# Issue order of DMAs in two recurrent scan layers: pinned loads and writes, a corner block in two parts on two queues, a block's older rows loaded first

## The chip, the cores and the metric

The kernel runs on one core of a Trainium2 chip. The metric is the device time of one execution in microseconds (us). The engines are TensorE (PE, matrix multiplications), VectorE (DVE), ScalarE (ACT), GpSimd (POOL) and SyncE (SP). SP and ACT also issue DMAs, each from its own queue: an issue that waits holds up everything behind it in the same queue.

## The reference, cut to what matters

The input is (4, 48, 256, 256) in float32: batch, channels, rows, columns. Four residual layers follow one another; the change touches the last two, which have the same form:

```python
def layer(x):                                   # layers 2 and 3 of the reference
    v = gn(x)                                   # group norm, 16 groups
    # conv1d: width 5, 48 channels to 48, along the other axis, with a bias
    # down: rows 0 to 255
    D[0] = v[:, :, 0];  D[h] = v[:, :, h] + conv1d(D[h - 1], down_w)
    # up: back over D, with the same weights; the last row of D stands in twice
    seq = rows 253, 252, ..., 0 of D, then row 255
    U = scan over seq from D[255], then reversed
    # right: columns 0 to 255 of U;  left: back over R
    R[0] = U[..., 0];   R[w] = U[..., w] + conv1d(R[w - 1], right_w)
    L[255] = R[255];    L[w] = R[w] + conv1d(L[w + 1], left_w)
    return x + L
```

Each layer is thus four chains of 255 steps, and a step needs the one before it.

## The kernel before, in words

The function `scans` does both scan layers; in its loop `layer` is 0 and 1. Layers 0 and 1 of the reference lie ahead of it and are not touched.

**A step.** A row (or column) of the image is kept as three blocks of 128 partitions by 128 elements: 8 positions times 48 channels are 384 lines, and the 128 elements are 32 groups of positions times the batch of 4. `step` (matmuls at L1227, additions at L1233) computes the convolution as nine 128x128 matmuls in float32, each of which the profile records as two, and adds the bias and the new input by three DVE operations.

**Tiles.** Eight rows make one row tile `D[a]`, a from 0 to 31, 1.5 MB. Three ring buffers and three slots hold row tiles in turn; the last five stay in the chip's memory, all others are written to memory by SP (L1371) at the end of their row tile, and come back for the up scan (L1428). `R[t_]` are the tiles of eight columns in the right scan, written likewise and read back by ACT's queue (L1582) in the left scan. Two big tiles hold, in turn, a block's input `x`, the corner and column blocks `u` and `c`, and the stage `s`.

**Down.** The input of a row tile is made by `norms`: twelve scale-and-shift operations, on ACT at L1302 (for the very first row tile a part goes to DVE and POOL, L1300). It writes them straight into the ring that the row tile will use: the norms of D[a+1] are issued among the steps of row tile a. With three rings in turn, that ring is free when D[a-2] has been written to memory. The scale and shift come from the group norm's statistics: `bn_stats` at L1569 in layer 0's left scan, gathered at L1596, averaged by L1603 and L1610, a Sqrt at L1615, and `spread` at L1244. The input x of four row tiles is a block J. Block J+1 is loaded from row tile 4J on: in layer 0 by `load_x2` (12 transfers), in layer 1 by `load_y` (L1263), ten transfers of rows of 256 bytes, 6.3 MB. The ten pieces arise because a position's 48 channels can lie across two blocks of 128 partitions: 48, 48, 32, 16, 48, 48, 16, 32, 48 and 48 lines.

**Up, and the corner to right.** While the up scan runs, ACT copies every row into a column-ordered tile `u` (`keep_row`, L1383), and every 32 rows SP writes it to `U` (`write_U`, L1388, ten pieces). The right scan reads columns: `load_C` brings 32 columns of all rows. For the first 32 columns, rows 64 and up are loaded at row 40 (24 transfers, L1401), and the row block 32 to 63 (J0 = 1) at row 32 (three transfers, L1396). After the very last step the kernel writes the first 64 of the 512 elements per position of the last row block (ten pieces), loads them back (three transfers, L1396), writes the other 448, and loads the weights of left (L1211). POOL copies each column from `c` into place (`fetch`, L1444), and the first step of right waits for it.

**Left, and the crossing to layer 1.** In the left scan POOL adds each finished column to the residual in the stage tile (`add_line`, L1512). In layer 0 the stage is written to `Y1` by `write_Y` (L1517), a block n of 32 columns at a time, n falling from 7 to 0; for n = 0 it is done in two parts, the first 64 elements of each position (through SP, ACT, SP), then the other 448. Layer 1's first block needs all of Y1's blocks for its 32 rows: `look_ahead` issues the part of n = 1 to 7 (56 rows of 256 bytes per line) as soon as a big tile is free and block 1 is written, and the part of n = 0 (8 rows per line) comes after the first corner write, over both queues. In layer 1 the finished stage goes to `out` (L1558).

**What sets the order.** The code is handed to a scheduler that orders each engine's instructions by its own reckoning of readiness. `pin = tc.keep_in_program_order` marks those instructions that must keep the order in which the program issues them; before the change these are the matmuls and additions of `step`, and norms and copies, but no DMA. A DMA of SP or ACT is therefore placed by the scheduler, which can differ from the program: the transfers of row 32 and the weights of left, for instance, stand in SP's queue ahead of the corner's writes. All DMAs of both queues share eight semaphores in turn, so that each also waits for the one eight before it.

Of the kernel before, what the change touches and what calls it, by code (L numbers as in the profile page):

```python
# [10 lines left out]
AF = mybir.ActivationFunctionType  # L11
# [5 lines left out]
B, C, H, W = 4, 48, 256, 256  # L17
# [9 lines left out]
NPOS = 8  # L27
# [1125 lines left out]
def scans(ctx, tc, x2r, out, wts, biases, dram, k, coef2, spare):  # L1153
# [16 lines left out]
    nc = tc.nc  # L1170
# [13 lines left out]
    pieces = pieces_of_lines()  # L1184
    chunk = lambda m: slice(128 * m, 128 * m + 128)

    NBK = 8
    pin = tc.keep_in_program_order
# [8 lines left out]
    def big_tile(name):  # L1197
        return big_of.take(name)
# [5 lines left out]
    ways = [(layer, way) for layer in range(2) for way in range(3)]  # L1204
    weights = {}

    def load_weights(at):
        if at < len(ways):
            layer, way = ways[at]
            t = wp.tile([128, 9, 128], F32, tag="w", name="w")  # L1210
            nc.sync.dma_start(t.rearrange("p a b -> p (a b)"), wts[layer][way])  # L1211
            weights[layer, way] = t

    def step(w, bias, old, new, inp, then=()):
# [43 lines left out]
    def load_y(t, J, n0=0, n1=NBK, queues=(nc.sync,)):  # L1258
        v = t.rearrange("p (m q e) -> p m q e", m=3, e=64)
        src = Y1.rearrange("q c e -> c q e")  # L1260
        for q, (j, c0, c1, m, p0, np_) in enumerate(pieces):
            at = 512 * j + 64 * J
            queues[q % len(queues)].dma_start(  # L1263
                v[p0 : p0 + np_, m, 8 * n0 : 8 * n1], src[c0:c1, 8 * n0 : 8 * n1, at : at + 64]
            )

    load_x2(xin, 0)
# [2 lines left out]
    both = (nc.sync, nc.scalar)  # L1270
    coefs = spread(coef2[:C].rearrange("p b s -> p (b s)"), "spread0")

    for layer in range(2):
        bias = b_sb[layer]
        w = weights[layer, 0]
        slot_of_row = (lambda i: (i % 2) * 4 + i // 2) if layer == 0 else (lambda i: i)
        U = dram.tile([NPOS, 3 * 128, NBK, NBK * 64], F32, tag=f"U{layer}", name="U")
        Dd = [dram.tile([128, RING], F32, tag=f"D{layer}_{a}", name="D") for a in range(32)]
        Rd = [dram.tile([128, RING], F32, tag=f"R{layer}_{a}", name="R") for a in range(32)]
        flat = lambda t: t.rearrange("p i m n -> p (i m n)")  # L1280
# [59 lines left out]
        for a in range(32):  # L1340
            t, h = D[a]
            J, al = a // 4, a % 4
            if al == 0:
                if J > 0:
                    give(xin_h)
                    xin, xin_h = xnext
                if J + 1 < NBK:
                    xnext = big_tile("x")
                    if layer == 0:
                        load_x2(xnext[0], J + 1)  # L1350
                    else:
                        load_y(xnext[0], J + 1)
            todo = []
            if a + 1 < 32:
                D[a + 1] = ring_tile("d")
                todo = norms(D[a + 1][0], xin if al < 3 else xnext[0], (al + 1) % 4)
            if layer == 0 and al == 0:
                copy_rows(xin, J)
            if a == 24:
                load_weights(ways.index((layer, 1)))  # L1360
            for i in range(NPOS):
                line = t[:, slot_of_row(i)]
                if prev is not None:
                    step(w, bias[:, 0], prev, line, line)
                prev = line
                for piece in todo[3 * i // 2 : 3 * (i + 1) // 2]:
                    piece()
                if copies and i % 2 == 0:
                    copies.pop(0)()
            if a < 32 - KEEP:  # L1370
                nc.sync.dma_start(Dd[a], flat(t))  # L1371
                give(D.pop(a)[1])
        give(xin_h)

# [3 lines left out]
        ut = uh = None  # L1378
        near = None
# [2 lines left out]
            v = t.rearrange("p (m i n a) -> p m i n a", m=3, i=NPOS, a=4)  # L1382
            nc.scalar.copy(v[:, :, i, :, al], line)  # L1383

        def write_U(t, J, lo, hi):
            v = t.rearrange("p (m i e) -> p m i e", m=3, i=NPOS)
            for j, c0, c1, m, p0, np_ in pieces:
                nc.sync.dma_start(  # L1388
                    U[j].rearrange("(i c) J e -> c i J e", c=C)[c0:c1, :, J, lo:hi], v[p0 : p0 + np_, m, :, lo:hi]
                )  # L1390

        def load_C(t, n, J0, J1):
            v = t.rearrange("p (m j J e) -> p m j J e", m=3, j=NPOS, J=NBK)
            for m in range(3):
                if J1 - J0 == 1:
                    nc.sync.dma_start(  # L1396
                        v[:, m, :, J0, :], U[:, chunk(m), J0, n * 64 : n * 64 + 64].rearrange("j f e -> f j e")
                    )
                    continue
                for j in range(NPOS):  # L1400
                    nc.sync.dma_start(v[:, m, j, J0:J1, :], U[j, chunk(m), J0:J1, n * 64 : n * 64 + 64])  # L1401

        for a in reversed(range(32)):
            t, h = D.pop(a)
            for i in reversed(range(NPOS)):
# [5 lines left out]
                if row % 32 == 31:  # L1411
                    ut, uh = big_tile("u")
# [7 lines left out]
                if row == 40:  # L1420
                    near = big_tile("c")
# [6 lines left out]
                nc.sync.dma_start(flat(D[a - KEEP][0]), Dd[a - KEEP])  # L1428
        step(w, bias[:, 0], prev, last, last)
        keep_row(ut, 0, 0, last)  # L1430
        write_U(ut, 0, 0, 64)
        load_C(near[0], 0, 0, 1)
        write_U(ut, 0, 64, 512)
        give(uh)
        load_weights(ways.index((layer, 2)))


        w = weights[layer, 1]
# [24 lines left out]
        for t_ in range(32):  # L1463
            n, gl = t_ // 4, t_ % 4
            if t_ > 0:
                R[t_] = ring_tile("r", (slot_of, ring_of) if t_ in (24, 25, 26, 30, 31) else (ring_of, slot_of))
            t, h = R[t_]
            if gl == 0 and n + 1 < NBK:
                near = big_tile("c")
# [12 lines left out]
            if t_ < 32 - KEEP:  # L1482
                nc.sync.dma_start(Rd[t_], flat(t))
                give(R.pop(t_)[1])
        load_weights(ways.index((layer, 2)) + 1)


        w = weights[layer, 2]
# [25 lines left out]
        def write_Y(s, n, lo=0, hi=512, queues=(nc.sync,)):  # L1514
            dst = Y1.rearrange("(n i) c e -> n (i c) e", n=NBK)[n, :, :SLOT].rearrange("f (j e) -> f j e", j=NPOS)
            for m in range(3):
                queues[m % len(queues)].dma_start(  # L1517
                    dst[chunk(m), :, lo:hi], s[m].rearrange("p (j e) -> p j e", j=NPOS)[:, :, lo:hi]
                )

        stages = {NBK - 1: stage_of(NBK - 1)}
        if layer == 0:
# [12 lines left out]

        look_ahead()
        for t_ in reversed(range(32)):
            n, gl = t_ // 4, t_ % 4
            t, h = R.pop(t_)
            for j in reversed(range(NPOS)):  # L1540
                wc = 8 * t_ + j
                wl = wc % 32
                line = t[:, j]
                then = [stats.pop(0)] if stats else []
                if wc < 255:
                    step(w, bias[:, 2], prev, line, line, then)
                prev = line
                add_line(stages[n][0], wl, line)
                if done and not stats:
                    for hh in done.pop(0):  # L1550
                        give(hh)
                    look_ahead()
                s, hs = stages[n]
                if layer == 1 and wl < NPOS and (wl % 2 == 0 or wc < 2):
                    to = 1 if wc < 2 else 2
                    for m in range(3):
                        here = slice(512 * wl, 512 * (wl + to))
                        nc.sync.dma_start(out[n, chunk(m), here], s[m][:, here])  # L1558
                    if wl == 0:
                        for hh in hs:  # L1560
                            give(hh)
                if layer == 0 and wl % 16 == 0:
                    half = wl // 16
                    for m in range(3):
                        for b in range(B):

                            def stat(m=m, b=b, s=s, at=2 * n + half, half=half):
                                v = s[m].rearrange("p (q b e) -> p q b e", b=B, e=16)[:, :, b]
                                return nc.vector.bn_stats(parts[:, m, b, at, :], v[:, :, 8 * half : 8 * half + 8])  # L1569

                            stats.append(stat)
                    if half == 0:
                        if n > 0:
                            write_Y(s, n)
                            written.append(n)
                        done.append(hs)
            give(h)
            look_ahead()
            while ring_of.free and min(R, default=t_) > 0:
                new = min(R, default=t_) - 1  # L1580
                R[new] = ring_tile("r")
                nc.scalar.dma_start(flat(R[new][0]), Rd[new])  # L1582
        for f in stats:
            f()
        if layer == 0:
# [11 lines left out]
            mean = work.tile([C, 2 * B], F32, tag="mean", name="mean")  # L1597
            av = k["avg24", 128].rearrange("p (m c) -> p m c", m=3)

            def average(src, dst, cols):  # L1600
                ps = small.tile([C, B], F32, tag="small", name="pavg")
                for m in range(3):
                    nc.tensor.matmul(ps, lhsT=av[:, m], rhs=src[:, m], start=m == 0, stop=m == 2)  # L1603
                return ps
# [6 lines left out]
            dev = work.tile([128, 3, B], F32, tag="dev", name="dev")  # L1611
            nc.vector.tensor_sub(dev, mv[:, :, :, 0], ps)
            nc.vector.tensor_mul(dev, dev, dev)
            nc.vector.tensor_add(dev, dev, mv[:, :, :, 1])
            nc.scalar.activation(mean[:, B:], average(dev, None, B), AF.Sqrt, bias=k.eps[:C])  # L1615
            nc.vector.reciprocal(gc[:, :, 0], mean[:, B:])
            nc.vector.scalar_tensor_tensor(gc[:, :, 1], mean[:, :B], -1.0, gc[:, :, 0], ALU.mult, ALU.mult)
            coefs = spread(gc.rearrange("p b s -> p (b s)"), "spread1")
# [167 lines left out]
```

## Time and profile before

| what | value |
|---|---|
| three runs | 6930.88, 6943.6, 6946.01 us; median 6943.6 |
| the profiled execution | 6936.42 us, its span 6934.4 |
| PE busy | 6569.4 us (95% of the span), 55772 matmuls recorded |
| DVE, ACT, POOL busy | 3636.3, 1844.0, 2069.2 us |
| scan matmuls at L1227 | 18360 records on d at 276 ns each, 18360 on r at 276 ns |
| additions at L1233 | 348 ns each |
| stages (us of the span) | layer 0: down and up 2614.6 to 3641.0, corner to 3659.5, right and left to 4729.6; crossing to 4775.4; layer 1: down and up to 5881.4, corner to 5900.6, right and left to 6927.4 |

The span runs from the first to the last instruction recorded; the execution's own time has 2.0 us more around it. In an answer of the timeline each line gives the start in us, the time in us, the engine, the line of the kernel, the operation with output and input by the program's names, and how many. "SPq" and "ACTq" stand for the queue of an engine: there the time is how long issues took, not how long the transfers did. The chain is followed back from the last instruction: at each step to what released it. A busy PE is not a PE at its peak, and idle time on an engine that is not on the chain costs nothing.

### The profile page before, as it was taken

How to read it: one execution, taken by the hardware profiler on the slowest of the kernel's cores; microseconds unless marked ns; L12 is line 12 of the kernel's file. 1: busy time of each engine (PE TensorE's matmuls, PEld its weight loads, DVE VectorE, ACT ScalarE, POOL GpSimd, SP SyncE). 2: the span in 40 equal slices, each digit the busy share in tenths (PEclk: the TensorE clock that was granted, in tenths of full speed). 3: DMA queues.
4: the chain of work that ended last, by engine and by line, in shares of the span. 5: the costliest groups of instructions: out<-in, count | busy, mean ns of one | idle time of the engine just before them, and what ended most of it. 6: DMA issues, size and time to landing. Idle time of an engine off the chain costs nothing.

```text
span 6934.4 us, 133567 instructions
## 1 busy us (share of the span) xinstructions
PE 6569.4 (95%) x55772; PEld 5266.6 (76%) x55772; DVE 3636.3 (52%) x8740; ACT 1844.0 (27%) x2166; POOL 2069.2 (30%) x4211
## 2 busy tenths in 40 slices
PE   6999999999999779999998999986899999999999
PEld 4666633333333229999998999986899999999999
DVE  7777533555556554444444446754444444444444
ACT  3430022444444434444440000001544443000000
POOL 0000000233333554420004557652000000555777
PEclk9999999999999879999999999998999999999999
DMA  7742145677777769984669678989995566865775
GB/s 237 185 136 84 61 133 176 165 199 195 196 199 184 158 148 301 287 245 155 187 179 226 195 172 205 248 243 188 182 183 95 170 195 171 235 186 168 276 300 201
DMA packets 1177469, 1326.21 MB, mean 191 GB/s; under 512 B 831040, under 2 KB 1005760, under 8 KB 1124512
## 3 DMA queue, kind: packets, MB, share of 16 engines
q1 hardware_dynamic: 1163696, 1229.16, 65.4%
q10 hardware_dynamic: 13072, 88.18, 3.7%
q8 instruction: 437, 7.16, 0.4%
q14 instruction: 168, 1.38, 0.1%
q0 software_dynamic: 96, 0.33, 0.0%
HBM read 794.28 MB, written 522.19 MB: 190 GB/s over the span
## 4 chain that ended last, share of the span: by engine, by line
PE 86%; DVE 4%; DMA 3%; SPq 2%; ACT 2%; POOL 1%; issue 1%; ACTq 0%; POOLq 0%; DVEq 0%
PE ps L1227 57%; PE py L701 9%; PE acc L374 8%; PE py L710 5%; SPq L1263 2%; PE ph L830 2%; PE pout L1018 1%; PE psp L975 1%; DMA D<-d 1%; ACT d L1302 1%; POOL s L1512 1%; PE ptok L890 1%; DVE y L724 0%; DVE st L726 0%; DVE y L1027 0%
## 5 line engine op out<-in xcount | busy, mean ns | idle before, releaser
L1227 PE MATMUL ps<-d,w 128*128 128x128 f32 (+1 forms) x18360 | 2073.8, 276 | 104.3 <-DVE d L1233 61.1
L1227 PEld LDWEIGHTS ps<-d,w 128*128 128x128 f32 x18360 | 2069.2, 193 | 108.8 <-DVE d L1233 64.7
L1227 PE MATMUL ps<-r,w 128*128 128x128 f32 (+1 forms) x18360 | 2066.7, 276 | 68.7 <-POOL r L1444 36.0
L1227 PEld LDWEIGHTS ps<-r,w 128*128 128x128 f32 x18360 | 2064.6, 193 | 70.9 <-POOL r L1444 37.0
L1233 DVE SCALAR_TENSOR_TENSOR d<-ps,b,d 128x128 f32<-128x128 f32 x3054 | 979.7, 348 | 1155.4 <-PE ps L1227 1077.2
L1512 POOL TENSOR_TENSOR s<-s,r 128x128 f32<-128x128 f32 x1536 | 745.4, 521 | 334.3 <-DVE r L1233 331.0
L1233 DVE SCALAR_TENSOR_TENSOR r<-ps,b,pre 128x128 f32<-128x128 f32 x1530 | 490.3, 348 | 577.1 <-PE ps L1227 569.0
L1233 DVE SCALAR_TENSOR_TENSOR r<-ps,b,r 128x128 f32<-128x128 f32 x1530 | 490.1, 348 | 459.1 <-PE ps L1227 431.4
L374 PE MATMUL acc<-moving,raw 128*32 128x240 f32 (+1 forms) x6144 | 685.6, 381 | 12.3 <-DVE moving L357 11.5
L1444 POOL COPY pre<-c 128x128 f32<-128x128 f32 x1530 | 558.4, 404 | 464.3 <-DVE r L1233 462.5
L701 PE MATMUL py<-x1n,wy 128*96 128x512 f32 x1536 | 691.6, 599 | 0.0
L374 PE MATMUL acc<-moving,still 128*32 128x240 f32 (+1 forms) x6144 | 682.5, 381 | 6.8 <-DVE still L361 2.7
L1302 ACT ACTIVATE d<-x,spread 128x256 f32<-128x256 f32 x752 | 510.9, 824 | 550.2 <-DMA D<-d 380.6
L1383 ACT COPY u<-d 128x384 f32<-128x384 f32 x510 | 448.5, 900 | 573.5 <-DVE d L1233 541.0
L374 PEld LDWEIGHTS acc<-moving,raw 128*32 128x32 f32 x6144 | 430.0, 110 | 213.6 <-DVE moving L357 11.8
L701 PEld LDWEIGHTS py<-x1n,wy 128*96 128x96 f32 x1536 | 242.0, 163 | 410.8 <-issue 376.3
L1444 POOL COPY r<-c 128x128 f32<-128x128 f32 x6 | 2.4, 393 | 1691.2 <-DMA c<-U 1691.2
L724 DVE TENSOR_TENSOR y<-py,t 96x512 f32<-96x512 f32 x256 | 173.6, 678 | 462.1 <-PE py L710 462.0
L374 PEld LDWEIGHTS acc<-moving,still 128*32 128x32 f32 x6144 | 345.0, 110 | 34.7 <-issue 4.6
L710 PE MATMUL py<-x2n,wy 64*96 64x512 f32 x1536 | 360.8, 601 | 0.0
L1034 POOL COPY yr<-y 96x256 f32<-96x256 f32 x512 | 307.2, 648 | 129.4 <-DVE y L1027 128.4
L654 ACT ACTIVATE x1n<-t,g 128x2048 f32<-128x2048 f32 x64 | 134.2, 2096 | 696.1 <-PE py L701 573.9
(219 smaller groups left out, 4076.2 us busy)
## 6 DMA issues: line engine op xcount, KB each, us to landing
t<-in_xc SPq DMA_DIRECT2D x64, 1536.0 KB
c<-U SPq DMA_DIRECT2D x348, 256.0 KB
D<-d SPq DMA_DIRECT2D x54, 1536.0 KB
d<-D SPq DMA_DIRECT2D x54, 1536.0 KB
R<-r SPq DMA_DIRECT2D x54, 1536.0 KB
r<-R ACTq DMA_DIRECT2D x54, 1536.0 KB
U<-u SPq DMA_DIRECT2D x84, 768.0 KB
raw<-in_xp SPq DMA_DIRECT2D x36, 1728.0 KB
```

Source lines behind the costliest of these rows:

```text
L374: nc.tensor.matmul(out[32 * i : 32 * i + 32, : n * C], lhsT=still[i][:, first : first + 32], rhs=moving[:, i, lo : lo + n * C], start=u == ...
L701: nc.tensor.matmul(ps, lhsT=held["w"][0][:, dx], rhs=x1n[:, 2 * c : 2 * c + 2, dx : dx + W], start=dx == 0, stop=False)
L710: nc.tensor.matmul(held["ps"][q + 2 * s], lhsT=held["w"][1][here, dx], rhs=x2n[here, 2 * q : 2 * q + 2, dx : dx + W], start=False, stop=dx ...
L724: nc.vector.tensor_add(part, held["ps"][c], t1[:P, 2 * c : 2 * c + 2, :])
L830: nc.tensor.matmul(out[32 * q : 32 * q + 32], lhsT=w1_sb[:, half, i, :], rhs=moving(t), start=i < 4, stop=i >= 4)
L1034: made = nc.gpsimd.tensor_copy(yrs[c][:, :, 2 * i2 + ip, :].rearrange("p j (n a g) -> p j n a g", a=4, g=4)[:, :, :, al], y[:, i2, al].rea ...
L1227: nc.tensor.matmul(ps[m][:, here], lhsT=w[:, n, :], rhs=old[:, q, there], start=first, stop=last)
L1233: nc.vector.scalar_tensor_tensor(new[:, m], ps[m], bias[:, m : m + 1], inp[:, m], ALU.add, ALU.add)
L1302: pin(nc.scalar.activation(dst, src, AF.Identity, bias=g[:, 1:2], scale=g[:, 0:1]))
L1383: nc.scalar.copy(v[:, :, i, :, al], line)
L1444: nc.gpsimd.tensor_copy(dst[:, m].rearrange("p (J a b) -> p J a b", J=NBK, b=B), v[:, m, j, :, gl].rearrange("p J b a -> p J a b"),)
L1512: nc.gpsimd.tensor_add(v, v, line[:, m].rearrange("p (J a b) -> p J a b", J=NBK, b=B))
```

## The change

The change adds `pin` to a number of DMA issues and moves some of them. Weights: every `load_weights` is pinned; left's are issued in tile 2 of the right scan instead of ahead of it, and the next layer's in tile 29 of the left scan instead of ahead of it. Corner: `write_U` and the three-transfer form of `load_C` are pinned; the last writes go over SP and ACT in turn; the load that follows them is in two parts, positions 0 and 1 over ACT, SP, ACT, then positions 2 to 7 over SP, ACT, SP. Layer 1's down scan: the pieces of `load_y` and, in layer 1 alone, the D writes are pinned, so that SP issues them as the program has them: the ten pieces for block J+1 at the start of row tile 4J, then the write of D[4J] at its end. Crossing: the 56-row pieces, the writes of n = 0 and the 8-row pieces are pinned in the program's order, and so is the Sqrt of the statistics, which stands behind ACT's pieces there. In the pinned order the three transfers for the row block 32 to 63 go out at row 32, as the program has it.

```diff
@@ load_weights
-            nc.sync.dma_start(t.rearrange("p a b -> p (a b)"), wts[layer][way])
+            pin(nc.sync.dma_start(t.rearrange("p a b -> p (a b)"), wts[layer][way]))
@@ load_y
-            queues[q % len(queues)].dma_start(
-                v[p0 : p0 + np_, m, 8 * n0 : 8 * n1], src[c0:c1, 8 * n0 : 8 * n1, at : at + 64]
+            pin(
+                queues[q % len(queues)].dma_start(
+                    v[p0 : p0 + np_, m, 8 * n0 : 8 * n1], src[c0:c1, 8 * n0 : 8 * n1, at : at + 64]
+                )
             )
@@ down scan, end of a row tile
             if a < 32 - KEEP:
-                nc.sync.dma_start(Dd[a], flat(t))
+                made = nc.sync.dma_start(Dd[a], flat(t))
+                if layer == 1:
+                    pin(made)
                 give(D.pop(a)[1])
@@ write_U
-        def write_U(t, J, lo, hi):
+        def write_U(t, J, lo, hi, which=pieces, queues=(nc.sync,)):
             v = t.rearrange("p (m i e) -> p m i e", m=3, i=NPOS)
-            for j, c0, c1, m, p0, np_ in pieces:
-                nc.sync.dma_start(
-                    U[j].rearrange("(i c) J e -> c i J e", c=C)[c0:c1, :, J, lo:hi], v[p0 : p0 + np_, m, :, lo:hi]
+            for q, (j, c0, c1, m, p0, np_) in enumerate(which):
+                pin(
+                    queues[q % len(queues)].dma_start(
+                        U[j].rearrange("(i c) J e -> c i J e", c=C)[c0:c1, :, J, lo:hi], v[p0 : p0 + np_, m, :, lo:hi]
+                    )
                 )
@@ load_C
-        def load_C(t, n, J0, J1):
+        def load_C(t, n, J0, J1, j0=0, j1=NPOS, queues=(nc.sync,)):
             v = t.rearrange("p (m j J e) -> p m j J e", m=3, j=NPOS, J=NBK)
             for m in range(3):
+                queue = queues[m % len(queues)]
                 if J1 - J0 == 1:
-                    nc.sync.dma_start(
-                        v[:, m, :, J0, :], U[:, chunk(m), J0, n * 64 : n * 64 + 64].rearrange("j f e -> f j e")
+                    pin(
+                        queue.dma_start(
+                            v[:, m, j0:j1, J0, :],
+                            U[j0:j1, chunk(m), J0, n * 64 : n * 64 + 64].rearrange("j f e -> f j e"),
+                        )
                     )
                     continue
@@ after the last step of up
         keep_row(ut, 0, 0, last)
-        write_U(ut, 0, 0, 64)
-        load_C(near[0], 0, 0, 1)
+        write_U(ut, 0, 0, 64, pieces, both)
+        load_C(near[0], 0, 0, 1, 0, 2, both[::-1])
+        load_C(near[0], 0, 0, 1, 2, NPOS, both)
         write_U(ut, 0, 64, 512)
         give(uh)
-        load_weights(ways.index((layer, 2)))
@@ right scan, end of a tile
-        load_weights(ways.index((layer, 2)) + 1)
+            if t_ == 2:
+                load_weights(ways.index((layer, 2)))
@@ write_Y
-                queues[m % len(queues)].dma_start(
+                made = queues[m % len(queues)].dma_start(
                     dst[chunk(m), :, lo:hi], s[m].rearrange("p (j e) -> p j e", j=NPOS)[:, :, lo:hi]
                 )
+                if n == 0:
+                    pin(made)
@@ left scan
         for t_ in reversed(range(32)):
+            if t_ == 29:
+                load_weights(ways.index((layer, 2)) + 1)
@@ statistics for layer 1
-            nc.scalar.activation(mean[:, B:], average(dev, None, B), AF.Sqrt, bias=k.eps[:C])
+            pin(nc.scalar.activation(mean[:, B:], average(dev, None, B), AF.Sqrt, bias=k.eps[:C]))
```

## The prediction

> **What bounds the kernel now.** I read the page's chain first, for who sets the end.
>
> ```profile
> PE 86%; DVE 4%; DMA 3%; SPq 2%; ACT 2%; POOL 1%; issue 1%; ACTq 0%; POOLq 0%; DVEq 0%
> PE ps L1227 57%; PE py L701 9%; PE acc L374 8%; PE py L710 5%; SPq L1263 2%; PE ph L830 2%; PE pout L1018 1%; PE psp L975 1%; DMA D<-d 1%; ACT d L1302 1%; POOL s L1512 1%; PE ptok L890 1%; DVE y L724 0%; DVE st L726 0%; DVE y L1027 0%
> ```
>
> The end is PE's: 57% are the scan steps of L1227, which no edit touches (9172 matmuls fill 1026.45 us of the first down and up scan: 2.01 us a step, 16.1 a row tile). Only waits between stretches of steps can change. By PE's stretches over the two scan layers those near the change are: the corner between up and right, 18.4 us (3641.0 to 3659.45) and again 19.1 (5881.4 to 5900.55); the crossing from layer 0 to layer 1, 45.8 (4729.6 to 4775.43); and the stalls of layer 1's down scan, 70.8 in all. The chain through the first corner (start, us, what):
>
> ```profile
> 3641.03 0.36 SPq L1211
> ...
> 3644.77 0.85 SPq L1388
> ...
> 3649.75 2.23 DMA U<-u
> ...
> 3652.62 5.05 DMA c<-U
> 3657.67 0.38 POOL r L1444
> ...
> 3659.45 15.56 PE ps L1227 x123
> ```
>
> The weights and the column loads of block 1 (L1396) go out ahead of the corner's own writes, ten writes follow one by one, and the load waits for the last. Then SP's queue from the crossing on:
>
> ```profile
> 4729.64 1.94 SPq L1517 DMA_DIRECT2D Y<-s  x2
> 4731.80 37.88 SPq L1263 DMA_DIRECT2D x<-Y  x15
> 4769.73 4.79 SPq L1517 DMA_DIRECT2D Y<-s  x3
> 4791.91 0.34 SPq L1371 DMA_DIRECT2D D<-d  x1
> 4792.41 49.41 SPq L1263 DMA_DIRECT2D x<-Y  x10
> 4841.94 7.69 SPq L1371 DMA_DIRECT2D D<-d  x3
> 4849.69 41.00 SPq L1263 DMA_DIRECT2D x<-Y  x10
> ...
> 4914.29 0.38 SPq L1263 DMA_DIRECT2D x<-Y  x1
> 4929.92 0.32 SPq L1371 DMA_DIRECT2D D<-d  x1
> 4930.29 39.73 SPq L1263 DMA_DIRECT2D x<-Y  x9
> ```
>
> A block's load holds SP for 30 to 49 us, and the next D write stands behind it. ACT's waits say who pays (line, releaser: total us, times, longest):
>
> ```profile
> ACT d L1302 <- DMA D<-d: 272.3, 13, 48.5
> ```
>
> The norms of row tile a+3 take the ring that D(a) leaves, so PE stalls at rows 4, 11, 15, 19, 23 and 27: 23.3, 13.4, 1.0, 14.5, 0.9, 17.7 us. From issue of the held D write to the row's first unbroken step are 23.0 us (4841.94 to 4864.95), likewise 23.0 and 23.3 behind loads of odd J, 20.9 and 20.2 behind even.
>
> **1. Corner, twice.** Removed from the path: weights (now issued in right's row tile 2, behind the R write, when their buffer has long been free) and the three L1396 issues of block 1 (now at row 32, some 64 us before up's end: hidden; without that cover 3.1 us return). Together 3641.03 to 3644.73: 3.7 us. ACT's copy of the last row ends at 3642.29, so writes start about 3642.4. Ten of them took 4.98 us (3644.77 to 3649.75); five on each queue take 2.5. The 448-column piece that stood before the load goes behind it: 0.5 us, inside the ten's following wait, not counted. The load's first part (2 of 8 positions) needs only the first two U pieces, on U's first index: issued by 3643.3, plus 2.2 landed at 3645.5, while the other eight still go out to 3645. Its three issues take about 0.4 each, and its landing lies between the 2.23 of a small write and the 5.05 of the full load. I take 2.9: the write plus a quarter of the difference, since a quarter of the bytes moves. So c part 1 is there at about 3648.4, then POOL 0.38 and start 0.1: PE at 3648.9. Gain 10.5; two corners 21. Bounds for each: 7 (loads slow each other, 5.05 stays, POOL waits for the second part) to 12.
>
> Here a rule speaks against the edit. The Trainium skill, "DMA: Bandwidth & Descriptors", section "Issuing engines are not separate DMA queues": DMAs of several issuers interleave on the same 16 engines, and a second issuer saves only issue time, usually small beside the transfer. In this trace it is not small: 4.98 us of issues against 2.23 of landing. By the rule as a habit the split brings nothing and each corner gains about 8; by the row it brings 2.5. The row is from this very place, I take it; 5 us of the sum hang on it.
>
> **2. Crossing.** Before, SP waits 51.3 us at L1517 for POOL's last add, and all fifteen loads of SP stand behind (37.9 us); x lands at 4772.3 while the coefficients were ready near 4748.4 (Sqrt at 4746.0, spread matmuls to 4748.2). After, the 56-row pieces go first. As built, the DMAs of SP and ACT share eight semaphores and each waits for the one eight before. So piece 1 starts when n=1's Y writes have landed (about 4702), pieces 3 to 7 after the R load (4712.68), pieces 8 to 10 after ACT's corner write (issued 4730.12, landed near 4732.3). Those three are a third of the bytes: of about 25 us that the ten took to issue and drain, 8. SP's two corner writes stand behind, landing about 4745 to 4747. Ten 8-row loads on two queues, 0.67 us each, to 4750; the Sqrt is now behind ACT's five of them: 4749.8, so coefficients are late next, 4752.5 (2.4 us as before); norms as before 3.1 (4772.34 to 4775.43): PE at 4755.6. Gain 20. Ends: 24 if only the coefficients decide (4748.4+3.1), 12 if the three pieces drain like the slow L1263 issues (about 3.4 us each, and their tail). The early pieces also run beside the R load that PE waits for at 4706.55 to 4712.68: up to 3 us lost, inside these ends.
>
> **3. Layer 1's down scan.** With loads and D writes pinned, the load of block J+1 is issued whole before D(4J). Before, D(0) went ahead of load 1, loads 3 to 7 had their first piece out one row earlier (4914.29 against 4929.92), and load 2 started right behind D(1) to D(3), 15 us before row 4. All three are lost.
> - Row 3: load 1 waits for the 448-column Y writes (5.4 MB, at the 405 GB/s seen there 13 us: landing about 10 us into the scan, where before load 1 began at 17). Ten pieces 44.7 (39.73 for nine, plus 5), D(0) then, and 23.0: row 3 at 78, row 4 at 94.5 us into the scan; before 89.5. Loss 5.
> - Row 7: load 2 begins at row 4's start. An even load took 30.35 for nine pieces, so about 34.4; plus 0.4 and 20.5 is 55.3, where three rows take 48.4: loss 7 (3 to 13: nine-piece time, or the 41.00 of load 2, which had three D writes in it).
> - Loads 3 to 7: one piece more in front of D(4J). Odd between 4.4 (a ninth of the time) and 5.7 (a seventh, as the first piece is 48 of 384 lines): 5. Even 3.4 to 4.3: 4. Three odd, two even: 23.
> Sum 35, bounds 10 (the early piece was worth nothing) to 74 (load 1's 49.41 less 39.73, so 9.7, and 41.00 less 30.35, so 10.6, as the piece's price; rows 3 and 7 at 10 and 13).
>
> **4. Nothing.** Weights for left and for the next layer move a few rows inside scans of 514 us; the start of layer 0 exchanges x0's first piece and two small loads, under 2 us either way; up, right and left keep their DMA order.
>
> **Sum.** 6936.4 (span 6934.4 and 2.0 around it) - 21 - 20 + 35 = 6930. The profiled execution lies 7 us under the median of 6943.6, inside the runs' 6931 to 6946. I keep the sum; against the median it is -0.2%.
>
> **Rivals.**
> A, the sum: 6930, its own range 6915 to 6948.
> B, the early piece was worth nothing, since a first piece issues in 0.38 us into idle queues and a load's time is set by what it meets (30 to 49 us for equal bytes): loss 10, time 6905. Against it: nine pieces do hold SP 40 us, longer than any wait shown within them.
> C, on the slower side: D(4J) behind the whole load at the price of the loads' differences, 9.7 and 10.6 each. Loss 74, time 6969. It decides from a loss of about 55. For it: the SP queue's own rows; against it: 49.41 and 41.00 had D writes inside them.
> D, the crossing does not gain: the R load is delayed, or pieces 8 to 10 hold the corner writes as long as before. It then gains 5, time 6945: no change.
>
> **How the numbers follow.** About 0.2% (14 us) is what a measurement of this kernel can tell from no change. A has 0.45, of which 0.22 faster, 0.18 within, 0.05 slower, since it lies on the bound; B 0.27, faster; C 0.20, slower; D 0.08, within. So faster 0.49, same 0.26, slower 0.25. The range reaches B's 6905 and A's upper bound with D and the mildest of C: 6902 to 6962.
>
> **What would show it.** Corner: PE idle of about 8 us between up and right, ten U writes on two queues, first c landing about 7 us after the last step. Crossing: L1263's 56-row pieces before 4729 on SP, PE idle about 26 us. Down scan: stalls at rows 3 and 7 (about 30 and 7 us) in place of row 4, and odd stalls near 18. If those odd stalls stay at 13 to 14, B is right; if they reach 23, C. The prediction is wrong if R loads or stage loads of left come later than before, as then stalls would grow where I see none.

## The result, and the profile after

The changed kernel takes 6957.03 us (median of 20 runs, 6942.52 to 6967.75) where the kernel before takes 6939.19 (20 runs, 6925.26 to 6946.01): a ratio of 1.0025, with a 95% interval of 1.0018 to 1.0032. It is 18 us slower. The forecast was 6930, faster than before; the time lies inside the forecast's range of 6902 to 6962, but on the other side of the kernel before. The profiled execution of the changed kernel has a span of 6948.9 us, 14.5 more than the 6934.4 of before.

TensorE's stretches on the matmuls of L1227 in the changed kernel show all places at once (start, us, how many; in brackets the idle time before, and what ended it):

```profile
2609.55 1026.43 PE L1227 MATMUL ps<-d,w 128*128 128x124 f32 x9172 [3.76 <-POOL d L1302]
3644.09 884.82 PE L1227 MATMUL ps<-r,w 128*128 128x128 f32 x7902 [8.11 <-POOL r L1454]
...
4700.94 16.52 PE L1227 MATMUL ps<-r,w 128*128 128x128 f32 x126 [12.10 <-DVE r L1233]
...
4742.52 50.40 PE L1227 MATMUL ps<-d,w 128*128 128x128 f32 x432 [3.30 <-ACT d L1304]
4816.45 0.79 PE L1227 MATMUL ps<-d,w 128*128 128x128 f32 x2 [23.54 <-DVE d L1233]
...
4822.16 65.30 PE L1227 MATMUL ps<-d,w 128*128 128x124 f32 x568 [1.21 <-DVE d L1233]
...
4894.25 66.48 PE L1227 MATMUL ps<-d,w 128*128 128x124 f32 x568 [1.19 <-DVE d L1233]
4977.74 0.80 PE L1227 MATMUL ps<-d,w 128*128 128x128 f32 x2 [17.01 <-DVE d L1233]
...
4983.43 66.27 PE L1227 MATMUL ps<-d,w 128*128 128x124 f32 x568 [1.21 <-DVE d L1233]
...
5310.75 593.05 PE L1227 MATMUL ps<-d,w 128*128 128x124 f32 x5284 [1.21 <-DVE d L1233]
5911.60 1031.01 PE L1227 MATMUL ps<-r,w 128*128 128x128 f32 x9180 [7.79 <-POOL r L1454]
```

The kernel before has these two lines at the start of layer 1 and at row tile 27:

```profile
4775.43 66.20 PE L1227 MATMUL ps<-d,w 128*128 128x128 f32 x576 [27.21 <-ACT d L1302]
...
5288.22 593.17 PE L1227 MATMUL ps<-d,w 128*128 128x124 f32 x5284 [1.18 <-DVE d L1233]
```

Stage by stage, from such lines of both profiles:

| stage | before, us | after, us | difference | forecast |
|---|---|---|---|---|
| start of the scans in the span | 2614.6 | 2609.6 | -5.0 | 0 |
| corner, layer 0 | 18.4 | 8.1 | -10.3 | -10.5 |
| right and left, layer 0 | 1070.1 | 1073.4 | +3.3 | up to +3, counted with the crossing |
| crossing (4729.5 to 4775.4; 4717.5 to 4742.5) | 45.9 | 25.1 | -20.8 | -20 |
| layer 1, start to row tile 27's unbroken steps | 512.8 | 568.2 | +55.4 | +35 |
| rest of down and up | 593.2 | 593.1 | 0 | 0 |
| corner, layer 1 | 19.1 | 7.8 | -11.4 | -10.5 |
| right and left, layer 1 | 1027.8 | 1031.0 | +3.2 | 0 |

The 5 us at the start lie in layers ahead of the scans; the kernels below, which share these layers, start theirs anywhere between 2606 and 2625, so these 5 us are left out of account. What remains is 14.5 + 5.0 = 19.5 us, close to the 17.8 between the medians.

So the gains came as forecast, and one loss was twenty larger. Here is the corner's chain after (start, us, what):

```profile
3636.40 0.87 ACT u L1387
...
3637.30 0.38 ACTq L1393
...
3637.72 0.48 ACTq L1393
...
3638.23 3.42 DMA U<-u
...
3641.68 1.99 DMA c<-U
3643.66 0.38 POOL r L1454
...
3644.09 5.98 PE ps L1227 x37
```

The weights, the old column loads and the issues of most of the ten writes have left it. And SP's queue from the crossing on:

```profile
4687.32 37.85 SPq L1264 DMA_DIRECT2D x<-Y  x10
4725.27 5.20 SPq L1528 DMA_DIRECT2D Y<-s  x2
4734.00 2.51 SPq L1264 DMA_DIRECT2D x<-Y  x5
4737.21 4.63 SPq L1528 DMA_DIRECT2D Y<-s  x3
4753.63 44.46 SPq L1264 DMA_DIRECT2D x<-Y  x10
4798.26 39.47 SPq L1373 DMA_DIRECT2D D<-d  x4
4837.78 36.44 SPq L1264 DMA_DIRECT2D x<-Y  x10
4874.33 36.92 SPq L1373 DMA_DIRECT2D D<-d  x4
4911.31 48.84 SPq L1264 DMA_DIRECT2D x<-Y  x10
4960.26 39.96 SPq L1373 DMA_DIRECT2D D<-d  x4
```

The older rows stand ahead of the corner writes, and the order that the prediction described is there: ten pieces, then four D writes. But load 3 (4911.31) takes 48.84 us, where its nine pieces had taken 39.73. Piece by piece, load 3 in the chain of the changed kernel:

```profile
4911.31 0.42 SPq L1264
...
4911.78 7.33 SPq L1264
...
4919.15 7.21 SPq L1264
...
4926.40 4.35 SPq L1264
...
4930.80 1.62 SPq L1264
```

The pieces have 48, 48, 32, 16 and 48 lines. A piece's issue is as long as the piece ahead of it is large: the second and third (7.33, 7.21) come behind pieces of 48 lines, the fourth (4.35) behind 32, the fifth (1.62) behind 16. The next four fit this too (7.70, 7.61, 2.61 and 4.91 behind 48, 48, 16 and 32 lines); the tenth, 4.67 behind 48 lines, is shorter than it should be. It looks as if an issue waits until the piece ahead has nearly gone, but no run tests this by itself. Sent early, the first piece has gone before the other nine come, and the second then issues at once (0.42 us): the early piece of before thus saved about 7.3 us of SP's time here, not its share of an average.

### The profile page after: what moved, and what is told of

The parts are those of the page before. It is cut to its first block, busy times and chain, and to the rows that moved or that the text cites. A ratio compares the mean times of both kernels' runs of the same rounds, so it can differ in the third digit from the quotient of the medians.

```text
span 6948.9 us, 133584 instructions
## 1 busy us (share of the span) xinstructions
PE 6579.8 (95%) x55772; PEld 5286.1 (76%) x55772; DVE 3637.1 (52%) x8740; ACT 1844.5 (27%) x2166; POOL 2069.2 (30%) x4211
## 4 chain that ended last, share of the span: by engine, by line
PE 86%; DVE 4%; DMA 2%; SPq 2%; ACT 2%; POOL 1%; issue 1%; ACTq 0%; POOLq 0%; DVEq 0%
PE ps L1227 57%; PE py L701 9%; PE acc L374 8%; PE py L710 5%; SPq L1264 2%; PE ph L830 2%; PE pout L1018 1%; PE psp L975 1%; ACT d L1304 1%; DMA D<-d 1%; DVE y L1027 1%; POOL s L1523 1%; PE ptok L890 1%; DVE y L724 0%; DVE st L726 0%
## 5 line engine op out<-in xcount | busy, mean ns | idle before, releaser
L1227 PE MATMUL ps<-d,w 128*128 128x128 f32 (+1 forms) x18360 | 2083.6, 277 | 126.0 <-DVE d L1233 106.6
L1227 PEld LDWEIGHTS ps<-d,w 128*128 128x128 f32 x18360 | 2077.2, 194 | 132.2 <-DVE d L1233 111.9
L1227 PE MATMUL ps<-r,w 128*128 128x128 f32 (+1 forms) x18360 | 2068.6, 276 | 51.7 <-DVE r L1233 35.8
L1227 PEld LDWEIGHTS ps<-r,w 128*128 128x128 f32 x18360 | 2065.1, 193 | 55.1 <-DVE r L1233 38.7
```

The lines of the kernel that those rows point to most:

```text
L1227: nc.tensor.matmul(ps[m][:, here], lhsT=w[:, n, :], rhs=old[:, q, there], start=first, stop=last)
```

## Experiments

**The down scan's order, alone and left out.** Two kernels split the change. The first is the changed kernel without the pins on the loads of blocks 1 to 7 and on D:

```diff
-            pin(
-                queues[q % len(queues)].dma_start( ... )
-            )
+            made = queues[q % len(queues)].dma_start( ... )
+            if J == 0:
+                pin(made)
...
-                made = nc.sync.dma_start(Dd[a], flat(t))
-                if layer == 1:
-                    pin(made)
+                nc.sync.dma_start(Dd[a], flat(t))
```

> The changed kernel with the down scan of layer 1 left to the scheduler again: the loads of blocks 1 to 7 and the D writes are not pinned; corner, weights and crossing as changed. Theory P (the pinned order alone makes the loss): the first 28 row tiles of layer 1 take about 513 us again instead of 568, the time is 55 us below the changed kernel, 37 below the kernel before (about 6902). Rival Q (the earlier crossing makes the loss, as the loads of the down scan now meet other transfers): the 28 row tiles still take over 540 us, and the time is at most 25 us below the changed kernel.

Measured: 6906.62 us (6902.1 to 6908.47), 0.9954 of before (0.994 to 0.9969). The first 28 row tiles take 518 us, from the first of these lines to the second:

```profile
4750.50 66.51 PE L1227 MATMUL ps<-d,w 128*128 128x128 f32 x576 [3.28 <-ACT d L1304]
...
5268.73 592.52 PE L1227 MATMUL ps<-d,w 128*128 128x124 f32 x5284 [1.21 <-DVE d L1233]
```

The second is the kernel before with only these pins:

```diff
-            queues[q % len(queues)].dma_start( ... )
+            made = queues[q % len(queues)].dma_start( ... )
+            if J > 0:
+                pin(made)
...
-                nc.sync.dma_start(Dd[a], flat(t))
+                made = nc.sync.dma_start(Dd[a], flat(t))
+                if layer == 1:
+                    pin(made)
```

> The kernel before with one part of the change: the loads of blocks 1 to 7 and layer 1's D writes pinned in program order. Theory P: about 50 to 55 us slower than before (6990), row tile 27 about 90 us after row tile 23, where it was 81; corners stay at 18 to 19 us. Rival Q: less than 30 us slower.

Measured: 6990.08 us (6987.15 to 6997.91), 1.0077 of before (1.0062 to 1.0092). Its 28 row tiles take 566 us:

```profile
4784.98 50.27 PE L1227 MATMUL ps<-d,w 128*128 128x128 f32 x432 [26.79 <-ACT d L1304]
...
5351.30 592.21 PE L1227 MATMUL ps<-d,w 128*128 128x124 f32 x5284 [1.21 <-DVE d L1233]
```

Against the 6937.51 that both share, the two parts are -30.9 and +52.6, sum +21.7, where the whole change has +17.8. Theory P holds, and Q falls: the pinned order makes the loss whatever the crossing does.

**The early piece given back.** In layer 1 the next big tile is taken one row tile earlier, since the norms have read the old block by then, and the first piece goes out ahead of D:

```diff
-            if al == 0:
+            if layer == 0 and al == 0:
...
+            if layer == 1:
+                if al == 3 and J + 1 < NBK:
+                    give(xin_h)
+                    xin, xin_h = xnext
+                to = J + 1 + (al == 3)
+                if to < NBK:
+                    if al == 3 or a == 0:
+                        xnext = big_tile("x")
+                    q0, q1 = ({0: (0, 10)} if to == 1 else {3: (0, 1), 0: (1, 10)}).get(al, (0, 0))
+                    load_y(xnext[0], to, q0=q0, q1=q1)
```

> The changed kernel, all pinned, but the first of the ten pieces of loads 2 to 7 goes out one row tile earlier, ahead of the D write. If the piece costs its own time on SP, 7.3 us behind odd loads (the issue that waits for a 48-line piece to drain) and 5 behind even ones: odd blocks 8 to 9 us shorter each, even ones 5, together 35 to 40 below the changed kernel, about 6920. If the loads are longer for another reason (the pinned D writes meeting them): less than 15 below.

Measured: 6909.35 us (6897.4 to 6924.75), 47.7 below the changed kernel: the piece costs its own time on SP, and more than the 35 to 40 expected. The order is still pinned. SP's queue has the rows of before again:

```profile
4890.38 0.32 SPq L1266 DMA_DIRECT2D x<-Y  x1
4904.65 0.32 SPq L1383 DMA_DIRECT2D D<-d  x1
4905.02 39.70 SPq L1266 DMA_DIRECT2D x<-Y  x9
```

The 28 row tiles take 520.9 us (4743.41 to 5264.31). Of the 55 us lost, 47 are one 48-line piece, issued too late, in six loads. Some 8 us are left, most of them at row 3, where D(0) stands behind load 1.

**The loads spread.** If D is late because it stands behind a load, no load should be issued at one go. With the edit above and these cuts of the ten pieces:

```diff
-                    q0, q1 = ({0: (0, 10)} if to == 1 else {3: (0, 1), 0: (1, 10)}).get(al, (0, 0))
+                    q0, q1 = ({0: (0, 4), 1: (4, 7), 2: (7, 10)} if to == 1
+                              else {3: (0, 3), 0: (3, 5), 1: (5, 8), 2: (8, 10)}).get(al, (0, 0))
```

> The changed kernel, all pinned, but the ten pieces of a load are issued over four row tiles (3, 2, 3 and 2 of them, beginning one row tile earlier), with the D write of each row tile between them; load 1 over three (4, 3, 3). If the whole loss is D writes standing behind loads in SP's queue, the stalls behind loads 2 to 7 go altogether and about 25 us remain for load 1: the 28 row tiles take some 470 us, the time is 95 us below the changed kernel (6860), 80 below the kernel before. If the stalls come from the memory traffic itself, it is no better than the one with the early piece, about 6920.

Measured: 6833.35 us (6825.28 to 6835.64), 0.9848 of before (0.9833 to 0.9862): 124 us below the changed kernel, where 95 had been expected. TensorE in layer 1's down and up:

```profile
4749.90 67.51 PE L1227 MATMUL ps<-d,w 128*128 128x128 f32 x584 [3.31 <-ACT d L1306]
4825.05 961.89 PE L1227 MATMUL ps<-d,w 128*128 128x124 f32 x8596 [7.63 <-DVE d L1233]
```

One stall of 7.6 us is left of the 70.8 of before, and the 28 row tiles take 446.8 us. The same bytes move beside the same steps, so the amount of memory traffic was not what made PE wait: it was the place of D in SP's queue. The landing of the held write agrees: D(8), behind load 3, lands in 13.99 us in the changed kernel and in 13.84 in the kernel before; only its issue comes later.

**What makes odd loads slow.** Loads 1, 3, 5 and 7 hold SP for 44 to 50 us, loads 2, 4 and 6 for 36. Counted from the start of a source row, a block begins at a multiple of 256 bytes, odd blocks at an odd one. The first test lets each load fetch the block after its own, which changes the output:

```diff
-            at = 512 * j + 64 * J
+            at = 512 * j + 64 * (J if J == 0 else J % 7 + 1)
```

> The changed kernel, but in layer 1's down scan the load of block J fetches the block after it (load 7 block 1), so that the output is not the reference's; sizes, places in the chip's memory and order are the same, only the offset in each source row moves by 256 bytes. If the source offset (an odd or even multiple of 256 bytes) makes loads 3, 5 and 7 slow, loads 1, 3 and 5 now take 35 to 37 us of SP's queue and loads 2, 4 and 6 take 44 to 50; load 7 stays at 49. If it is what runs beside the load or which of the two buffers it fills, nothing changes: odd loads 49, even ones 36.

Measured: loads 1 to 7 take 44.6, 36.2, 49.3, 37.0, 48.8, 37.0 and 48.4 us; 6951.34 us in one run. The source offset is not it. The second test exchanges the two big tiles:

```diff
-    ring_of, slot_of, big_of = Slots(rings, RING), Slots(slots, SLOT), Slots(big, BIG)
+    ring_of, slot_of, big_of = Slots(rings, RING), Slots(slots, SLOT), Slots(big[::-1], BIG)
```

> The changed kernel with the two big tiles taken in the other order from the start, so that in layer 1 the loads of odd blocks fill the big tile that even ones filled, and the other way round. If the place in the chip's memory makes a load slow: loads 1, 3, 5 and 7 take 35 to 37 us of SP's queue, loads 2, 4 and 6 take 44 to 50. If it is the order in time, or what runs beside: no change, odd 49 and even 36.

Measured, in one run of 6943.83 us: the pattern turns over. Its loads 1 to 3 in SP's queue:

```profile
4764.28 31.91 SPq L1264 DMA_DIRECT2D x<-Y  x10
...
4832.35 47.52 SPq L1264 DMA_DIRECT2D x<-Y  x10
...
4920.15 35.62 SPq L1264 DMA_DIRECT2D x<-Y  x10
```

So it is the tile that a load fills. It shows ahead of the down scan too: SP's ten pieces of older rows at the crossing now fill the other tile, and take 46.00 us where they took 37.85. By the addresses that the build assigns, the first big tile begins at byte 20960 of every partition, the second at 176640. Two unused pads move both to multiples of 512 and leave the rings at one:

```diff
+    pool("c_pad0", 1).tile([128, 8], F32, tag="pad", name="pad0")
     big = [pool("c_big0", 1)]
...
+    pool("c_pad1", 1).tile([128, 120], F32, tag="pad", name="pad1")
     rings = [pool(f"c_ring{i}", 1) for i in range(3)]
```

> The changed kernel with two unused pads: 32 bytes per partition ahead of the first big tile, 480 ahead of the rings. As built before, the first big tile begins at byte 20960 of a partition, which is 32 past a multiple of 64, the second at 176640, a multiple of 512; with the pads both begin at multiples of 512 (20992 and 177152), and the rings again at one. If the odd loads are slow by the beginning of their rows in the chip's memory: all loads 35 to 37 us, rows 11, 19 and 27 each 10 to 13 us earlier, load 1 as in the run with the big tiles swapped, 32: the time falls by 35 to 50 us, to about 6910. If it is the tile's region and not its beginning: no change (6957, odd loads 49).

Measured, in one run: 6889.01 us, 68 below the changed kernel's median and more than the 35 to 50 expected. Loads 1 to 7 take 33.1, 35.8, 36.7, 36.8, 36.8, 36.8 and 36.4 us. Load 3, which took 48.84:

```profile
4894.30 36.65 SPq L1266 DMA_DIRECT2D x<-Y  x10
```

The 28 row tiles take 508.3 us (4741.34 to 5249.66), 60 less than the 568.2 of the changed kernel. The pads in the kernel before, its order untouched:

> The kernel before with the two pads alone, its order left as it was. If the stalls of rows 11, 19 and 27 (13.4, 14.5 and 17.7 us) are those of loads into the tile whose rows begin off a multiple of 64 bytes: they shrink to the 1 us of rows 15 and 23, load 1 is about 12 us shorter, corners and crossing stay: 45 to 55 us below the kernel before, about 6888. If the pinned order is needed for the gain: less than 15.

Measured: 6870.66 us (6860.29 to 6882.76), 0.9895 of before (0.9878 to 0.9912), 69 us below it. Its 28 row tiles take 455.2 us (4779.91 to 5235.07), 57.6 less than before; where the other 11 of the 69 lie was not looked for. Odd loads issue as even ones do (load 3, then load 4):

```profile
4918.81 30.59 SPq L1265 DMA_DIRECT2D x<-Y  x9
...
4984.12 31.21 SPq L1265 DMA_DIRECT2D x<-Y  x9
```

With both big tiles at such a beginning the pinned order costs 508.3 - 455.2 = 53 us in this stage, near the 55.4 without the pads. Two separate costs, then: the order in the queue, and the beginning of the rows.

The pads with the spread loads:

> The kernel with loads spread over four row tiles, with the same two pads. Its down scan has about 11 us of stalls left, and columns and stages are loaded into the same big tiles. If the beginning counts: 10 to 30 us below the spread kernel's 6833, as load 1 and left's stage loads get shorter too; if not: within 5 us of it.

Measured: 6824.1 us (6815.44 to 6831.52), 0.9838 of before (0.9819 to 0.9857). The median is 9 us below the spread kernel's and the lowest here, but the two kernels' runs overlap. The profile is plainer. Layer 1's down and up are one unbroken stretch:

```profile
4754.36 1027.71 PE L1229 MATMUL ps<-d,w 128*128 128x128 f32 x9180 [3.28 <-ACT d L1308]
```

From the scan's first step to up's last, the spread kernel took 1037.0 us (4749.90 to 5786.94): 7.6 of the 9.3 gained are the stall that was left. The gain is just short of the 10 to 30 expected. Left's waits stayed: 11.13 us before its last stretch, where the spread kernel had 11.65.

**The corner's two parts, each undone.** One queue for the corner's writes and loads:

```diff
-        write_U(ut, 0, 0, 64, pieces, both)
-        load_C(near[0], 0, 0, 1, 0, 2, both[::-1])
-        load_C(near[0], 0, 0, 1, 2, NPOS, both)
+        write_U(ut, 0, 0, 64)
+        load_C(near[0], 0, 0, 1, 0, 2)
+        load_C(near[0], 0, 0, 1, 2, NPOS)
```

> The changed kernel with the corner's ten writes and both parts of its load on SP's queue alone. If the issue time counts (4.98 us for ten on one queue): PE idle in each corner 10.5 to 11.5 us where it is 8.1. If a second queue saves nothing: 8.1 again.

```profile
3655.25 885.72 PE L1227 MATMUL ps<-r,w 128*128 128x128 f32 x7902 [9.42 <-POOL r L1454]
```

PE idles 9.42 us in place of 8.11, and 9.44 in place of 7.79 in layer 1: the second queue saves 1.3 to 1.7 us, less than the 2.4 or more that was expected, but not nothing: the profiled kernels with two queues and two parts idle 7.75 to 8.74 in these places. One part for the load:

```diff
-        load_C(near[0], 0, 0, 1, 0, 2, both[::-1])
-        load_C(near[0], 0, 0, 1, 2, NPOS, both)
+        load_C(near[0], 0, 0, 1, 0, NPOS, both)
```

> The changed kernel with the corner's load in one part of eight positions, over ACT and SP. If the part counts: the load waits for the last write and takes 4 to 5 us to land, PE idle 10 to 11 us in each corner where it is 8.1. If only the queues and the moved weights count: 8 to 8.5.

```profile
3654.12 2.08 PE L1227 MATMUL ps<-r,w 128*128 128x128 f32 x8 [11.14 <-POOL r L1453]
3656.83 884.16 PE L1227 MATMUL ps<-r,w 128*128 128x124 f32 x7894 [0.64 <-POOL r L1453]
```

PE idles 11.14 and once more 0.64, and in layer 1 11.24 and 0.67: the part saves 3.0 to 3.7 us in layer 0, 3.5 to 4.1 in layer 1. In its chain the load takes 3.57 us to land, where the first part took 1.99. The whole times of these two single runs (6965.19 and 6967.24) lie within the spread of the changed kernel and say nothing; the idle times do.

## Why the prediction was right or wrong

**Wrong in sign, by one term of the sum.** The gains were put at 41 us. The profile has 10.3 + 11.4 + 20.8 = 42.5, less the 3.3 in left, and with the down scan's pins left out the kernel is 31 us faster. The loss was put at 35 us and measured 55.4 in the profile and 52.6 by the pins alone. A forecast that sets two sums of 40 against each other needs both within a few us, and this one had its loss too small by twenty.

**The corner: the sum right, in part by luck.** 8.1 and 7.8 us of idle time were forecast as about 8, from 18.4 and 19.1. The second queue brought 1.3 to 1.7 us, not 2.5. The issues do not halve: five take 3.18 us on ACT and 2.99 on SP, of which 0.6 to 0.7 is a wait for the landing of an earlier write, where ten take 4.98 on SP alone. And the load's first part did not wait for its own two writes only. In the chain above its last transfer goes out at 3641.68, when the third write that ACT issued (at 3638.23) has landed after 3.42 us. That write holds position 4, and the part reads positions 0 and 1; but in the trace the two transfers use the same one of the eight semaphores. The prediction had reckoned with this ring at the crossing and not here: it had the write landed 4.5 us after the last step, and it was 5.7. The first part then took 1.99 us, not 2.9, and the two errors nearly cancelled. The rule that the prediction weighed, that issuing from a second queue saves only issue time (the Trainium skill, "DMA: Bandwidth & Descriptors", "Issuing engines are not separate DMA queues"), held: the issues got 1.8 us shorter (4.98 to 3.18), and no more than that was saved.

**The crossing: right.** PE idles 25.1 us, forecast 26. SP's own rows show the steps: the older rows issued by 4725.2, the two corner writes then, the ten 8-row loads at 4734, the Sqrt at 4737.0 behind ACT's five of them, and the coefficients late last (norms begin at 4739.47 on the spread). Counted from the end of left, each point came within about 1 us of the forecast: the corner writes landed at 16.5 us (15.5 to 17.5 forecast), the Sqrt began at 19.6 (20.3), PE at 25.1 (26.1). The R load in left took 9.03 us to land, not 6.13, and PE's wait there was 12.10, not 9.18: the 3 us that had been named as an end. Rival D, by which the crossing gains 5, is out.

**The down scan: the mechanism right, a size wrong.** Row 3 was forecast at 78 us into the scan and began its unbroken steps at 79.6; row 7, by the same steps, was forecast at 149.8 and began at 151.7. Counted from the end of one unbroken stretch to the start of the next, the stalls there are 29.2 and 6.8 us, forecast about 30 and 7. Those behind loads 3, 5 and 7 are 22.7, 24.2 and 25.7, where the prediction looked for 18 and had named 23 as the sign of rival C. The step that failed is "Loads 3 to 7: one piece more in front of D(4J)": 5 us for odd loads and 4 for even ones. From the issue of the D write ahead of a load to that of D(4J) behind it, odd loads grew from 40.2 to 49.3 (load 3), from 41.0 to 51.2 (load 5) and from 47.3 to 55.4 (load 7, with the weights between); even ones by 5.4 and 5.5. That is 38 us where the sum had 23, and the rest of the miss is small: of the 55.4 us, rows 3 and 7 took about 14 (forecast 12), which leaves 41 for loads 3 to 7. The working had spread the time of nine pieces evenly over them or over their lines. But an issue waits for the piece ahead, and the rows of single issues give its price. They stood in the trace of before, in load 1, whose ten pieces went out together; its second, third and fourth:

```profile
4792.78 7.52 SPq L1263
...
4800.34 8.36 SPq L1263
...
4808.74 3.41 SPq L1263
```

Behind a piece of 48 lines 7.5 and 8.4 us, then: for odd loads the moved piece costs over 7 us, not 5. The other 1 to 3 us of their growth are not split further.

**Rivals.** C had taken nearly that price for odd loads, 9.7, and was given 0.20; its price for even loads, 10.6, was twice what came. B, that the early piece was worth nothing, had 0.27 and is refuted by the early piece given back: 47.7 us. The sentence held against B, that nine pieces hold SP longer than any wait shown within them, was the better guide than the chance that it got.

**Nothing, forecast for the rest: nearly.** Layer 1's right scan lost 3.2 us. In the first half of it, two of PE's matmuls every 43 us start 0.25 and 0.21 us after the one ahead, where most start 0.11 after; in the kernel before there is one such start, of 0.21, every 129 us. Layer 1's right and left take 1029.8 to 1031.0 us in every profiled kernel with the corner in two parts and the moved weights, the one with the corner on one queue (1030.0) among them, and 1027.3 to 1027.9 in the three without. So it is not the second queue; which of the other edits makes it was not tried.

## What to carry to other kernels

A load of tens of us in an in-order queue is a wall for the small write that frees the next buffer: pin the order only together with a cut of the load, so that the write stands behind two or three pieces and not ten (here 446.8 us for 28 row tiles in place of 568.2). Price a moved piece by its own issue in the trace, not by its share of the whole. Before any reordering, look for two like transfers of unlike length, and compare where their rows begin: two unused pads were worth more here (69 us) than the corner and the crossing together (31).

## What the runs showed of the hardware that was not expected

A DMA of 256-byte rows into a tile that begins 32 bytes past a multiple of 64 (224 past a multiple of 256) holds the queue 48.8 us, and 36.7 us into the same tile moved 32 bytes on (load 3): a factor of 1.33 for 24,576 rows (384 lines of 64 rows). The Trainium skill, "DMA: Bandwidth & Descriptors", "How a descriptor splits into AXI transactions", says of a descriptor that does not start at a multiple of 256 bytes that its first transaction starts at the 256-byte boundary below, and that the bytes ahead of the start are fetched, not used, and still cost beats. An estimate by that page's counting, if a row is one descriptor: a row of 256 bytes that begins at 224 costs 15 beats and not 8, a factor of 1.9. The direction agrees, the size here is smaller, and the page describes reads, while these rows are written at the tile's side; that the same thing is at work there is not shown. Moving the source by 256 bytes, a multiple that keeps it on the grid, changed nothing (36.2 and 49.3 us for loads 2 and 3). Whether 64, 128 or 256 bytes is the grid that counts was not tried.
